# Probabilities of four heads laid out by key block, in an encoder-decoder on one core

## The chip, the cores and the metric

The kernel runs on one core of a Trainium2 chip. The metric is the device time of one execution in microseconds, the median over several runs. A profiled execution gives the trace: what each engine did and when. TensorE (PE) multiplies matrices and turns tiles, VectorE (DVE) and ScalarE (ACT) move results out of PSUM and compute on them, GpSimd (POOL) works on data in SBUF, SyncE (SP) issues DMAs.

## The reference

One encoder layer over a context of 77 tokens and one decoder layer over 2048 tokens, for two batches, width 512, 16 heads of 32, inner width 2048, all in fp32. The decoder layer is causal self-attention with a bias by relative position, cross-attention to the encoder's output, and a feed-forward net, each with a layer norm before it and a residual after it:

```python
y = y + _mha(yn, yn, dec_sa_in_w, dec_sa_in_b, dec_sa_out_w, dec_sa_out_b, sb)   # sb: bias + causal mask
y = y + _mha(_ln(y, dec_n2_s, dec_n2_b), memory, dec_ca_in_w, ..., cb)
h = _ln(y, dec_n3_s, dec_n3_b)
y = y + (jax.nn.relu(h @ dec_ff1_w.T + dec_ff1_b) @ dec_ff2_w.T + dec_ff2_b)
```

In `_mha` the scores of a head are q times k over the square root of 32, plus the bias; a softmax over the keys gives the probabilities; these times v give the head's output. The change touches the self-attention alone.

## The kernel before

**Two parts in time.** Until about 1720 us the kernel does the self-attention of both batches, with the encoder and the first cross-attention between. From there to the end it does the other cross-attentions and the feed-forward nets, with block matrices multiplied by a scheme of sums (L1376, L1405). All order is written out by hand: instructions reach each engine in the order in which the program calls them, and each engine works its queue in that order.

**Units.** The self-attention is cut into 128 units (b, m, g, t): batch, token block of 512 queries (m = 0 to 3), group of four heads, tile of 128 queries, numbered in that order, so 16 units make a token block. Unit (b, m, g, t) has m * 4 + t + 1 key blocks of 128 keys, since attention is causal: 1 to 4 in token block 0, 13 to 16 in token block 3. Units 16, 32 and 48 begin token blocks 1, 2 and 3 of batch 0; unit 64 begins batch 1, and 80, 96 and 112 its later blocks.

**A unit's steps.**

- *Scores* (`scores`, L374). A unit's key blocks go in pieces of up to four. A piece is one matmul for each of the four heads into its own PSUM bank, of the seven that go round (`bank`). VectorE moves each head's piece into the tile of probabilities `pp` and takes its maximum (L383); the last two key blocks of the unit get the bias on the way (L390).
- *Exponentials* (L400, L405). After the last piece the maxima are joined, and ScalarE does one exponential for each head, in place over all its key blocks. They are kept in a list (`late_exps`) and issued one by one at chosen places (`exps`).
- *Turns* (`turn`, L425). TensorE transposes each 128 x 128 tile of probabilities, four to a bank; ScalarE (L431) and VectorE (L429) copy the banks to SBUF. The turns of a unit go in groups of two pieces. In token block 0 four turns of one head's key blocks share a bank, elsewhere the four heads of one key block.
- *Values* (`values`, L442). The turned tiles times v, summed over the key blocks.

**Where the probabilities lie.** `pp` holds two units at once: units of even number from its start, of odd number up to its end (`probabilities`, L345). Each unit has room for (m + 1) * 512 keys for each of four heads. A head's row is contiguous: head r begins at r * (m + 1) * 512, so the places depend on m.

**The loop** (L1610). For each group of turns of unit n: if scores of n are still to be done, they are done; exponentials of n still in the list are issued; then the turns; then, behind the last group of a unit, the slot of the next one, which holds other work such as projections (L216, L227, L240) in a table by unit; then one score piece, if it may go; an exponential or two; the values; then more pieces as long as they may. `may_score` (L1593) decides whether the next piece of the stream may go. It takes the place of unit n - 2, the last of the same parity. Within one token block a piece waits only until those key blocks of n - 2 have been turned which it will write over. Where n - 2 lies in another token block or batch, it waits until all of n - 2 has been turned:

```python
same = n >= 2 and units[n][:2] == units[n - 2][:2]
return n < 2 or turned_to[n - 2] >= (min(k0 + kn, size[n - 2]) if same else size[n - 2])
```

**The ring of weights.** The last part's weights come through a ring of 16 tiles in the first half of `pp` (`w_ring`, L1271). `feed` fills it. Its first calls come during the turns of unit 126, the last of even number, for as many tiles as key blocks have been turned.

Of the kernel before, what the change touches and what calls it, by code (L numbers as in the profile page):

```python
# [12 lines left out]
ALU = mybir.AluOpType  # L13
# [4 lines left out]
P = 128  # L18
B, T, S, D = 2, 2048, 77, 512
# [3 lines left out]
HC = P // HD  # L23
MB = 512
NMB = T // MB
TB = MB // P
# [3 lines left out]
LOWEST = -3.0e38  # L30
# [24 lines left out]
def tile_encoder_decoder(ctx: ExitStack, tc: tile.TileContext, ins, out):  # L55
    nc = tc.nc
    x, src = ins["x"], ins["ctx_1024"]
# [10 lines left out]
    ident = const.tile([P, P], F32, name="ident")  # L68
# [90 lines left out]
    with (  # L159
# [9 lines left out]
        pp = ac.tile([P, 2 * HC * T], F32, name="pp")  # L169
# [10 lines left out]
        def bank():  # L180

            i = count["bank"] % count["banks"]
            count["bank"] += 1
            return psum[:, i, :]

        def in_turn(what, tile):
            i = count[what] % tile.shape[1]
            count[what] += 1
            return tile[:, i, :]

        def rows4(r):
            return slice(r * HD, (r + 1) * HD)


        nTs, qTs, ots, sums_of = {}, {}, {}, {}
# [134 lines left out]
        units = [(b, m, g, t) for b in range(B) for m in range(NMB) for g in range(NC) for t in range(TB)]  # L330
        stream = [(n, k0, kn) for n, u in enumerate(units) for k0, kn in pieces(u[1] * TB + u[3])]
        state = {}
        biases = {}
# [11 lines left out]
        def probabilities(n):  # L345
            w = (units[n][1] + 1) * MB
            at = END - HC * w if n % 2 else 0
            return [pp[:, at + r * w : at + (r + 1) * w] for r in range(HC)]

        late_exps = []  # L350

        def exps(k):

            for _ in range(min(k, len(late_exps))):
                late_exps.pop(0)[1]()

        def scores(n, k0, kn):
            b, m, g, t = units[n]
            i = m * TB + t
            if k0 == 0:  # L360
                state[n] = {
                    "p": probabilities(n),
                    "mx": sm.tile([P, HC, 8], F32, name="mx", tag="mx"),
                    "nm": sm.tile([P, HC], F32, name="nm", tag="nm"),
                    "col": 0,
                }
                if t == 0:
                    sums_of[b, m, g] = sm.tile([P, TB, HC], F32, name="sums", tag="sums")
            st = state[n]
            last = k0 + kn == i + 1  # L370
            q = qTs[b, m, g]
            banks = [bank() for _ in range(HC)]
            for r in range(HC):
                nc.tensor.matmul(  # L374
                    banks[r][:, : kn * P], q[rows4(r), ts(t, P)], kT[rows4(r), g, k0 * P : (k0 + kn) * P],
                    start=True, stop=True,
                )
            far = max(0, kn - 2) if last else kn
            col = st["col"]
            for r in range(HC):  # L380
                p, s, c = st["p"][r], banks[r], col
                if far:
                    nc.vector.tensor_scalar(  # L383
                        p[:, k0 * P : (k0 + far) * P], s[:, : far * P], 1.0, None, ALU.mult, ALU.max,
                        accum_out=st["mx"][:, r, c : c + 1],
                    )
                    c += 1
                if last:
                    w = (kn - far) * P
                    nc.vector.tensor_tensor_reduce(  # L390
                        p[:, (i + 1) * P - w : (i + 1) * P], s[:, far * P : kn * P],
                        biases[b, m, g][:, r, 2 * P - w :], 1.0, LOWEST, ALU.add, ALU.max,
                        accum_out=st["mx"][:, r, c : c + 1],
                    )
                    c += 1
            st["col"] = c
            if not last:
                return

            nc.vector.tensor_reduce(st["nm"], st["mx"][:, :, :c], AX.X, ALU.max, negate=True)  # L400
            for r in range(HC):
                p, nm, to = st["p"][r][:, : (i + 1) * P], st["nm"][:, r : r + 1], sums_of[b, m, g][:, t, r : r + 1]

                def run(p=p, nm=nm, to=to):
                    nc.scalar.activation(p, p, AF.Exp, bias=nm, accum_out=to)  # L405

                late_exps.append((n, run))
# [3 lines left out]
        def turn(pieces):  # L411

            first = units[pieces[0][0]][1] == 0
            loads = []
            for n, k0, kn in pieces:
                ks = range(k0, k0 + kn)
                if first:
                    loads += [[(n, k, r) for k in ks] for r in range(HC)]
                else:
                    loads += [[(n, k, r) for r in range(HC)] for k in ks]  # L420
            for o, load in enumerate(loads):
                pt = bank()
                pts = in_turn("pts", pts_all).rearrange("p (x q) -> p x q", q=P)
                for x, (n, k, r) in enumerate(load):
                    nc.tensor.transpose(pt[:, ts(x, P)], state[n]["p"][r][:, ts(k, P)], ident)  # L425
                    got[n, k, r] = pts[:, x, :]
                w = len(load) * P
                if o % 2 if first else o >= (len(loads) + 1) // 2:
                    nc.vector.tensor_copy(pts[:, : len(load), :], pt[:, :w])  # L429
                else:  # L430
                    nc.scalar.copy(pts[:, : len(load), :], pt[:, :w])  # L431
                if not first and o == min(3, len(loads) - 1):
                    exps(1)
            exps(HC if first else 1)
# [501 lines left out]
        for x, (b, m) in enumerate(blocks):  # L936
# [28 lines left out]
            for g in range(NC):  # L965
# [4 lines left out]
                at = u + g * TB - 3  # L970
# [78 lines left out]
        low, high = pp[:, : END // 2], pp[:, END // 2 :]  # L1049
# [208 lines left out]
        def weight_tiles():  # L1258
            for x in range(len(blocks)):
                for n in range(per):  # L1260
                    if x + 1 < len(blocks):
                        yield from cross_tiles(n)
                    if n < FIRST:
                        j, f = first_slots[n]
                        yield w1_tile(ONE[j][0], f)
                    else:
                        j, part = divmod(n - FIRST, 4)
                        for k in range(2 * part, min(2 * part + 2, 7)):
                            yield w2_d[ON_W2[TWO[j][1]], k]

        w_ring = [low[:, j % 4 * T + j // 4 * D : j % 4 * T + j // 4 * D + D] for j in range(16)]  # L1271
        tiles, fed, used = weight_tiles(), [0], [0]

        def feed(upto):
# [314 lines left out]
        size = [m * TB + t + 1 for b, m, g, t in units]  # L1589
        turned_to, scored_to, at = {n: 0 for n in range(end)}, {}, [0]  # L1590

        def may_score():

            if at[0] == len(stream):
                return False
            n, k0, kn = stream[at[0]]
            same = n >= 2 and units[n][:2] == units[n - 2][:2]
            return n < 2 or turned_to[n - 2] >= (min(k0 + kn, size[n - 2]) if same else size[n - 2])

        def score_next():  # L1600
            n, k0, kn = stream[at[0]]
            scores(n, k0, kn)
            scored_to[n] = k0 + kn
            at[0] += 1
# [4 lines left out]
        i = 0  # L1609
        while i < len(stream):  # L1610
            n = stream[i][0]
            pair = [p for p in stream[i : i + 2] if p[0] == n]
            while scored_to.get(n) != size[n]:
                score_next()
            while any(u == n for u, _ in late_exps):
                exps(1)
            ends = pair[-1][1] + pair[-1][2] == size[n]
            if ends:
                for f in ahead[n + 1]:
                    f()  # L1620
            turn(pair)
            if n == end - 2:
                for _, k0, _ in pair:
                    feed(k0 + 4)
            turned_to[n] = pair[-1][1] + pair[-1][2]
            if ends and n + 1 < end:
                slot(n + 1)
            if may_score():
                score_next()
            exps((0, 2, 1, 1)[units[n][1]])  # L1630
            for p in pair:
                values(*p)
            while may_score() and (len(pair) > 1 or units[n][1] == 0):
                score_next()
            i += len(pair)
# [67 lines left out]
```

## Time and profile before

| | |
|---|---|
| median of 3 runs | 2796.83 us (2796.19 to 2797.98) |
| profiled execution | 2796.27 us |
| its span | 2794.2 us |
| mean granted clock of TensorE | 0.997 |
| TensorE busy | 2764.6 us, 99% |
| VectorE busy | 1858.0 us, 66% |
| ScalarE busy | 1435.3 us, 51% |
| GpSimd busy | 875.6 us, 31% |

A row of a timeline gives the start, the length, the engine, the line, the operation, what it writes and reads, the shape of one, how many were merged, and in brackets how long the engine had been idle before and what released it. Rows of the same line that follow each other are merged, also when their shapes differ; the shape shown is that of the first. The profile lists a score matmul of L374 as two records, so a piece of four heads is x8. Ends of matmuls are modelled, and the distance between two starts is the safer measure. A row of windows gives a stretch, its length, and for each engine the busy time and the number of instructions, then the granted clock of TensorE and the load of the DMA engines. A row of groups gives the busy time in total, the mean length of one, and the idle time ahead of the group.

### The profile page before, as it was taken

Reading aid. Unit: us, or ns where it says so; the run is one execution under the profiler, and the core shown is the slowest. Engines: PE = TensorE matmul, PEld = TensorE weight load, DVE = VectorE, ACT = ScalarE, POOL = GpSimd, SP = SyncE. Lnnn points to the kernel's source line nnn. Section 1 sums busy time; section 2 is a strip of 40 time slices with the busy share of each in tenths; the row PEclk is TensorE's granted clock in tenths of the full one; section 3 lists DMA queues with packets and bytes.
Section 4 is the critical chain, followed back from the end, with each engine's and each line's share of the span. In section 5 each row is a group of like instructions: output and inputs, shape, how many; then the busy total and the mean of one; then the engine's idle time right before and its main releaser. Section 6 shows DMA issues by size and latency. Waiting matters only on the chain. (4 is left out here: it accounts for less than half of the span.)

```text
span 2794.2 us, 65938 instructions
## 1 busy us (share of the span) xinstructions
PE 2764.6 (99%) x25998; PEld 2076.6 (74%) x25998; DVE 1858.0 (66%) x5360; ACT 1435.3 (51%) x2751; POOL 875.6 (31%) x745
## 2 busy tenths in 40 slices
PE   9999999999999999999999999999999999999998
PEld 5567666666666556666666667898989898989898
DVE  5666587778887577687778885565555656464645
ACT  3544466656666556666646666434344444444431
POOL 0301143300100312122200001364747474746456
PEclk9999999999999999999999999999999999999999
DMA  6414344411112512232311014574747565656475
GB/s 194 116 56 135 111 143 123 139 31 48 38 41 73 140 47 70 84 107 92 106 33 39 26 50 134 174 242 145 237 152 236 175 226 163 223 162 220 148 226 181
DMA packets 281271, 355.31 MB, mean 127 GB/s; under 512 B 37968, under 2 KB 156544, under 8 KB 280834
## 3 DMA queue, kind: packets, MB, share of 16 engines
q1 hardware_dynamic: 280962, 351.10, 40.6%
q8 instruction: 206, 3.38, 0.5%
q14 instruction: 103, 0.84, 0.1%
HBM read 309.51 MB, written 41.49 MB: 126 GB/s over the span
## 5 line engine op out<-in xcount | busy, mean ns | idle before, releaser
L405 ACT ACTIVATE pp<-pp,nm 128x128 f32<-128x128 f32 (+15 forms) x512 | 612.0, 1203 | 137.2 <-DVE nm L400 136.8
L383 DVE TENSOR_SCALAR_CACHE_REDUCE pp<-psum 128x512 f32<-128x512 f32 (+3 forms) x1024 | 559.5, 591 | 64.0 <-PE psum L374 62.0
L431 ACT COPY pts<-psum 128x512 f32<-128x512 f32 (+3 forms) x592 | 300.5, 577 | 505.6 <-PE psum L425 369.7
L425 PEld LDWEIGHTS psum<-ident,pp 128*128 128x128 f32 x4352 | 473.1, 141 | 107.8 <-DVE pp L383 51.6
L425 PE MATMUL psum<-ident,pp 128*128 128x128 f32 x4352 | 533.6, 277 | 8.4 <-ACT pp L405 2.9
L429 DVE COPY pts<-psum 128x512 f32<-128x512 f32 (+2 forms) x544 | 330.0, 660 | 69.2 <-PE psum L425 67.7
L374 PE MATMUL psum<-kT,q 32*128 32x512 f32 (+3 forms) x2560 | 355.7, 576 | 5.2 <-DVE pp L383 2.6
L442 PEld LDWEIGHTS psum<-pts,vv 128*32 128x32 f32 x8704 | 225.6, 110 | 123.7 <-issue 115.8
L1405 PE MATMUL psum<-pp 128*128 128x128 f32 x2560 | 304.5, 276 | 1.9 <-POOL pp L1113 1.6
L1405 PEld LDWEIGHTS psum<-pp 128*128 128x128 f32 x2560 | 296.3, 192 | 8.6 <-issue 2.8
L442 PE MATMUL psum<-pts,vv 128*32 128x128 f32 x8704 | 278.2, 275 | 0.7 <-ACT pts L431 0.5
L1113 POOL TENSOR_TENSOR pp<-pp 128x512 f32<-128x512 f32 x159 | 212.5, 1353 | 111.1 <-DMA pp<-in_dec_ff_wT_dram 52.0
L1376 PE MATMUL psum<-vv,pp 128*128 128x256 f32 x1024 | 236.2, 381 | 0.0
L374 PEld LDWEIGHTS psum<-kT,q 32*128 32x128 f32 x2560 | 123.2, 183 | 140.7 <-issue 91.2
L1376 PEld LDWEIGHTS psum<-vv,pp 128*128 128x128 f32 x1024 | 190.3, 190 | 25.8 <-issue 0.5
L390 DVE CUSTOM_DVE_ANT_0 pp<-psum,bias 128x256 f32<-128x256 f32 (+1 forms) x512 | 196.0, 411 | 15.3 <-PE psum L374 15.2
L1389 DVE TENSOR_TENSOR kT<-kT,psum 128x512 f32<-128x512 f32 x96 | 65.8, 686 | 190.7 <-PE psum L1376 190.5
L1376 PE MATMUL psum<-nT,pp 128*128 128x256 f32 x768 | 174.1, 380 | 0.0
L1392 ACT ACTIVATE kT<-kT,vecs 128x256 f32<-128x256 f32 x192 | 87.0, 501 | 156.7 <-DVE kT L1389 156.0
L287 POOL TENSOR_TENSOR rstd<-rstd,mhalf 128x1 f32<-128x1 f32 x32 | 18.5, 578 | 458.7 <-DVE rstd L286 378.6
L1376 PEld LDWEIGHTS psum<-nT,pp 128*128 128x128 f32 x768 | 144.2, 190 | 20.3 <-issue 1.6
L470 POOL TENSOR_TENSOR oT<-rirows,oT 128x512 f32<-128x512 f32 x30 | 38.6, 1287 | 363.8 <-DMA rirows<-rec 187.8
(211 smaller groups left out, 3784.8 us busy)
## 6 DMA issues: line engine op xcount, KB each, us to landing
pp<-w_d SPq DMA_DIRECT2D x520, 256.0 KB
pp<-in_dec_ff_wT_dram SPq DMA_DIRECT2D x112, 256.0 KB
wqk<-in_dec_sa_in_wT_dram SPq DMA_DIRECT2D x64, 256.0 KB
bias<-tzg SPq DMA_DIRECT2D x128, 128.0 KB
pp<-wo_d SPq DMA_DIRECT2D x56, 256.0 KB
wbig<-in_dec_sa_in_wT_dram SPq DMA_DIRECT2D x8, 1024.0 KB
vv<-in_enc_ff_wT_dram SPq DMA_DIRECT2D x8, 1024.0 KB
xr<-in_x_dram SPq DMA_DIRECT2D x32, 256.0 KB
```

The source lines that it names most:

```text
L374: nc.tensor.matmul(banks[r][:, : kn * P], q[rows4(r), ts(t, P)], kT[rows4(r), g, k0 * P : (k0 + kn) * P], start=True, stop=True,)
L383: nc.vector.tensor_scalar(p[:, k0 * P : (k0 + far) * P], s[:, : far * P], 1.0, None, ALU.mult, ALU.max, accum_out=st["mx"][:, r, c : c + 1],)
L390: nc.vector.tensor_tensor_reduce(p[:, (i + 1) * P - w : (i + 1) * P], s[:, far * P : kn * P], biases[b, m, g][:, r, 2 * P - w :], 1.0, LOW ...
L405: nc.scalar.activation(p, p, AF.Exp, bias=nm, accum_out=to)
L425: nc.tensor.transpose(pt[:, ts(x, P)], state[n]["p"][r][:, ts(k, P)], ident)
L429: nc.vector.tensor_copy(pts[:, : len(load), :], pt[:, :w])
L431: nc.scalar.copy(pts[:, : len(load), :], pt[:, :w])
L442: nc.tensor.matmul(ot[rows4(r), t, :], vv[:, k, ts(g * HC + r, HD)], got.pop((n, k, r)), start=(k == 0), stop=(k == i),)
L1113: engine.tensor_tensor(out, a, b, ALU.subtract)
L1376: nc.tensor.matmul(mm[:, ts(f, TOK)], a[:, c, ts(f, P)], b[:, c, :], start=fresh and f == 0 and c == 0, stop=c == 1, skip_group_check=True,)
L1392: nc.scalar.activation(dst[:, e, :], src[:, e, :], AF.Relu, bias=vec("dec_ff1_b", f + e))
L1405: nc.tensor.matmul(psum[:, bank_i, ts(col, P)], lhs[:, c, :], w[:, c, :], start=fresh and k in (0, 3) and c == 0, stop=c == 3, skip_group_ ...
```

## The change

The probabilities of a unit are laid out by key block: key block k takes 512 adjacent places, 128 for each of the four heads side by side, so key block k of a unit of even number lies at k * 512 whatever the token block is. A unit of odd number still ends at the end of `pp`; when the token block grows by one, its key block k lies where key block k - 4 of the earlier unit lay, and when a new batch begins, where key block k + 12 lay. A head's row is then a row of runs of 128 elements, 512 apart, and the instructions that write or read it (L383, L390, L405) get an access pattern with one dimension more. The turns read the same 128 x 128 tiles at other places.

`may_score` has one rule for all units: a piece may go when the key blocks of unit n - 2 whose places it takes have been turned. For units of odd number at the start of a batch the shift is added (`moved`); where the token block grows, a piece waits for as many key blocks as before the shift. The slots of the ring of weights are now the 16 runs of 512 one after another, so that slot j takes the place of key block j.

```diff
         def probabilities(n):
             w = (units[n][1] + 1) * MB
             at = END - HC * w if n % 2 else 0
-            return [pp[:, at + r * w : at + (r + 1) * w] for r in range(HC)]
+            p = pp[:, at : at + HC * w].rearrange("p (k r x) -> p r k x", r=HC, x=P)
+            return [p[:, r] for r in range(HC)]
...
             for r in range(HC):
-                p, s, c = st["p"][r], banks[r], col
+                p, s, c = st["p"][r], banks[r].rearrange("p (k x) -> p k x", x=P), col
                 if far:
                     nc.vector.tensor_scalar(
-                        p[:, k0 * P : (k0 + far) * P], s[:, : far * P], 1.0, None, ALU.mult, ALU.max,
+                        p[:, k0 : k0 + far], s[:, :far], 1.0, None, ALU.mult, ALU.max,
                         accum_out=st["mx"][:, r, c : c + 1],
                     )
                     c += 1
                 if last:
-                    w = (kn - far) * P
+                    near = biases[b, m, g][:, r, :].rearrange("p (k x) -> p k x", x=P)
                     nc.vector.tensor_tensor_reduce(
-                        p[:, (i + 1) * P - w : (i + 1) * P], s[:, far * P : kn * P],
-                        biases[b, m, g][:, r, 2 * P - w :], 1.0, LOWEST, ALU.add, ALU.max,
+                        p[:, k0 + far : i + 1], s[:, far:kn], near[:, 2 - (kn - far) :], 1.0, LOWEST, ALU.add, ALU.max,
                         accum_out=st["mx"][:, r, c : c + 1],
                     )
...
             for r in range(HC):
-                p, nm, to = st["p"][r][:, : (i + 1) * P], st["nm"][:, r : r + 1], sums_of[b, m, g][:, t, r : r + 1]
+                p, nm, to = st["p"][r][:, : i + 1], st["nm"][:, r : r + 1], sums_of[b, m, g][:, t, r : r + 1]
...
-                    nc.tensor.transpose(pt[:, ts(x, P)], state[n]["p"][r][:, ts(k, P)], ident)
+                    nc.tensor.transpose(pt[:, ts(x, P)], state[n]["p"][r][:, k], ident)
...
-        w_ring = [low[:, j % 4 * T + j // 4 * D : j % 4 * T + j // 4 * D + D] for j in range(16)]
+        w_ring = [low[:, ts(j, D)] for j in range(16)]
...
             n, k0, kn = stream[at[0]]
-            same = n >= 2 and units[n][:2] == units[n - 2][:2]
-            return n < 2 or turned_to[n - 2] >= (min(k0 + kn, size[n - 2]) if same else size[n - 2])
+            if n < 2:
+                return True
+            moved = TB * max(0, units[n - 2][1] - units[n][1]) if n % 2 else 0
+            return turned_to[n - 2] >= min(k0 + kn + moved, size[n - 2])
```

## The prediction

> **What bounds the kernel now.** I read the page first, then the table of windows by unit, then TensorE's timeline around the changes of token block, and last the groups by form for the instructions whose access changes.
>
> ```profile
> span 2794.2 us, 65938 instructions
> ...
> PE 2764.6 (99%) x25998; PEld 2076.6 (74%) x25998; DVE 1858.0 (66%) x5360; ACT 1435.3 (51%) x2751; POOL 875.6 (31%) x745
> ```
>
> TensorE is never idle for long, so only time that it loses inside its own queue can be won. Its listed idle time hides some of this, because a matmul that waits in the pipe is drawn as a long one. So I compare like with like: the units of self-attention. A unit is one tile of 128 queries for one group of four heads; unit 48 is the first of token block 3 in batch 0, unit 112 the first of token block 3 in batch 1. A unit's window runs from its first turn (L425) to the next unit's.
>
> ```profile
> core 0: us, PE busy (x) PEld busy (x) DVE busy (x) ACT busy (x) POOL busy (x), PEclk, DMA share, GB/s
> ...
> 582.51:594.79 12.28, 12.28 (x152) 8.77 (x148) 7.06 (x24) 9.24 (x14) 0.00 (x0) 1.00 0.00 1
> ...
> 611.00:635.44 24.44, 22.88 (x225) 14.11 (x221) 20.00 (x62) 12.41 (x18) 1.29 (x1) 1.00 0.20 56
> 635.44:653.19 17.75, 17.75 (x212) 11.66 (x208) 15.21 (x50) 11.12 (x15) 0.00 (x0) 1.00 0.01 2
> ...
> 706.09:723.84 17.75, 17.75 (x212) 11.66 (x208) 16.23 (x53) 11.12 (x15) 3.88 (x3) 1.00 0.00 1
> ...
> 1450.14:1476.54 26.40, 24.84 (x225) 16.16 (x221) 20.08 (x62) 12.46 (x18) 1.29 (x1) 0.87 0.18 51
> ...
> 582.51:653.19 70.68, 69.07 (x764) 45.44 (x760) 55.82 (x176) 40.96 (x58) 1.29 (x1) 1.00 0.07 21
> 1421.65:1494.29 72.64, 71.03 (x764) 47.48 (x761) 55.91 (x176) 41.17 (x58) 1.29 (x1) 0.95 0.07 20
> ```
>
> The rows are units 46, 48, 49, 53 and 112, then units 46 to 49 and 110 to 113 together. Units 48 and 112 take 24.44 and 26.40 us where their neighbours take 17.75. Part of that is honest work: scores of unit 49 that could not be issued earlier. The rest is loss, and the next two fences price it. First a unit without a passage (52), as the price list; a cost is the distance between two starts, since the ends are modelled:
>
> ```profile
> 688.85 0.71 PE L374 MATMUL psum<-kT,q 32*128 32x256 f32 x8
> 689.49 3.71 PE L425 MATMUL psum<-ident,pp 128*128 128x128 f32 x32
> 693.14 1.14 PE L374 MATMUL psum<-kT,q 32*128 32x512 f32 x8
> 694.21 1.95 PE L442 MATMUL psum<-pts,vv 128*32 128x128 f32 x64
> ...
> 697.16 2.40 PE L425 MATMUL psum<-ident,pp 128*128 128x128 f32 x20
> 699.40 3.60 PE L216 MATMUL psum<-nT,wqk 128*128 128x512 f32 x8
> ...
> 705.23 0.93 PE L374 MATMUL psum<-kT,q 32*128 32x384 f32 x8
> ```
>
> So a score piece of four key blocks costs 1.07 us (693.14 to 694.21), of three 0.86 (705.23 to 706.09, where the next unit's window begins), of two 0.64 (688.85 to 689.49); 32 turns cost 3.65, 20 turns 2.24. Now the passage from unit 47 to 49:
>
> ```profile
> 592.93 1.14 PE L374 MATMUL psum<-kT,q 32*128 32x512 f32 x8
> ...
> 601.39 2.26 PE L374 MATMUL psum<-kT,q 32*128 32x384 f32 x16
> 603.58 1.97 PE L425 MATMUL psum<-ident,pp 128*128 128x128 f32 x16
> ...
> 611.00 0.55 PE L425 MATMUL psum<-ident,pp 128*128 128x128 f32 x3
> 612.78 3.38 PE L425 MATMUL psum<-ident,pp 128*128 128x128 f32 x29 [1.23 <-ACT pp L405]
> 616.09 1.14 PE L374 MATMUL psum<-kT,q 32*128 32x512 f32 x8
> ...
> 619.05 1.58 PE L374 MATMUL psum<-kT,q 32*128 32x512 f32 x14
> 620.96 5.14 PE L374 MATMUL psum<-kT,q 32*128 32x256 f32 x18 [0.33 <-DVE pp L383]
> 626.03 2.66 PE L425 MATMUL psum<-ident,pp 128*128 128x128 f32 x20
> 628.65 3.70 PE L240 MATMUL psum<-wbig,nT 128*128 128x512 f32 x8
> ```
>
> Four places lose time. (a) Two pieces in a row, of three and two blocks: 601.39 to 603.58 is 2.19 against 0.86 + 0.64 = 1.50, a loss of 0.69. (b) The first 32 turns of unit 48: 611.00 to 616.09 is 5.09 against 3.65, a loss of 1.44, and the row names the exponential. (c) Four pieces in a row (x14 and x18 records are 4 x 8; three of four blocks, one of two): 619.05 to 626.03 is 6.98 against 3 x 1.07 + 0.64 = 3.85, a loss of 3.13, and the row names VectorE's evacuation L383. (d) 20 turns: 2.62 against 2.24, a loss of 0.38. Together 5.64 us. The second passage has the same work and is longer by 72.64 - 70.68 = 1.96, so it loses 7.60. The extra is the clock:
>
> ```profile
> 1462.00:1470.00 8.00, 8.00 (x35) 6.12 (x34) 6.63 (x26) 2.15 (x4) 0.00 (x0) 0.57 0.01 2
> ...
> 1466.12 3.89 PE L425 MATMUL psum<-ident,pp 128*128 128x128 f32 x20
> 1469.85 3.60 PE L240 MATMUL psum<-wbig,nT 128*128 128x512 f32 x8
> ```
>
> Right behind the starved stretch the granted clock is 0.57 over 8 us, and the same 20 turns take 3.73.
>
> **The change part by part.** *Order.* Before, a piece of a unit in a new token block waited until the unit two earlier was turned completely; now it waits only for the key blocks whose place it takes. Following the loop of L1610 with both rules, the order differs at three places in 128 units. At 46 to 49, and alike at 110 to 113, unit 48's pieces 0 and 4 move from unit 47 into unit 46 (behind its first eight blocks of turns, around its products), piece 8 moves ahead of unit 47, piece 11 follows unit 47's turns, and unit 49's pieces 0 and 4 follow in unit 47, piece 8 ahead of unit 48. Unit 48 then has 49's last piece, 50's 0 and 4, each behind turns or products, which is the pattern of unit 52. At 62 to 64 unit 64's one block is scored a half unit earlier; no row there shows a wait for it, and I price it at nothing, hidden by unit 63's two groups of turns. The passages from block 0 to 1 and 1 to 2 do not change: those units have at most eight key blocks and turn them in one go, so there is no earlier moment. Nothing is added or removed: the same turns, pieces, products and projections lie between the start of unit 46 and that of unit 50, so the whole difference is loss removed.
>
> *Loss (c), (a) and (d).* They arise because VectorE gets several pieces at once:
>
> ```profile
> L383 DVE TENSOR_SCALAR_CACHE_REDUCE pp<-psum 128x512 f32<-128x512 f32 x672 | 422.8, 687 | 48.0 <-PE psum L374 47.4
> ...
> L383 DVE TENSOR_SCALAR_CACHE_REDUCE pp<-psum 128x256 f32<-128x256 f32 x128 | 53.8, 420 | 6.8 <-PE psum L374 6.8
> L383 DVE TENSOR_SCALAR_CACHE_REDUCE pp<-psum 128x384 f32<-128x384 f32 x96 | 47.8, 554 | 7.3 <-PE psum L374 6.2
> ...
> L816 DVE TENSOR_TENSOR pts<-psum,cmx 128x308 f32<-128x308 f32 x52 | 24.9, 479 | 2.3
> ...
> L1386 ACT COPY kT<-psum 128x512 f32<-128x512 f32 x96 | 57.4, 598 | 91.0 <-PE psum L1376 90.9
> ...
> L431 ACT COPY pts<-psum 128x512 f32<-128x512 f32 x544 | 283.2, 594 | 455.5 <-PE psum L425 325.7 <-DVE oT L448 71.7 <-issue 24.3
> ```
>
> A head's evacuation occupies 422.8 / 672 = 0.63 us, a piece of four heads 2.52, while TensorE makes it in 1.07; with seven banks TensorE is one and a half pieces ahead at most. Spread out, the same 55.82 us of VectorE in 70.68 become 55.82 / (70.68 - 5.64) = 86%, as in unit 49 (15.21 of 17.75, 86%) and below unit 53 (16.23 of 17.75, 91%), both without such a wait. Unit 46, where VectorE is only 7.06 of 12.28 busy, takes in three pieces in place of most of one (made from 592.93 on, so some 1.7 us of its evacuation lies before the window's end at 594.79): about 7.06 - 1.7 + 2 x 2.52 + 4 x 0.50 = 12.4 in 12.28 + 1.07 + 0.86 = 14.2 us, 87%. What is queued behind them there is one copy of turned blocks, and TensorE has a projection of 3.60 us to do meanwhile.
>
> *Loss (b).*
>
> ```profile
> 604.32 1.07 ACT L431 COPY pts<-psum 128x512 f32<-128x512 f32 x2 [6.78 <-PE psum L425]
> 605.95 1.68 ACT L405 ACTIVATE pp<-pp,nm 128x1664 f32<-128x1664 f32 x1 [0.56 <-DVE nm L400]
> ...
> 610.97 1.67 ACT L405 ACTIVATE pp<-pp,nm 128x1664 f32<-128x1664 f32 x1
> ```
>
> All four exponentials of unit 48 run between 605.95 and 612.64 and the turns of the fourth head wait for the last. With the new order the first of them is called before unit 47's last turns. Three are left, without the wait for the maxima: behind the two copies that end at 605.39 they are done near 605.4 + 3 x 1.67 = 610.4, and unit 48's turns begin at 611.0. That cover of 0.6 us is TensorE's projection and products between; if it is gone, the 1.44 comes back as far as it is short.
>
> *Layout.* Rows of probabilities become runs of 128 elements with a hop of 512. Turns still read 128 adjacent columns, so TensorE is untouched. For VectorE, L816 writes four runs of 77 (three hops): 479 ns, where the line between 420 (256) and 554 (384) gives 474 at 308. So 5 ns, 1.7 a hop. For ScalarE, L1386 writes two runs of 256: 598 against 594. With 13 to 16 runs in each of four exponentials that is at most 4 x 15 x 4 ns = 0.24 us a unit, on an engine busy 11.12 of 17.75. Both are hidden. Ends: nothing, and, at the other side, a hop as dear as an instruction of its own (rival 2). No gain is to be had from hops, since the element count stays. The ring of weights for the last stage gets other slots in the same half of the buffer, filled at the same four calls; a slot is one run of 512 either way, so nothing.
>
> *Sum.* 5.64 + 7.60 = 13.24 us at most. I leave 0.3 at each passage for small bank waits: 12.6. The profiled execution took 2796.27 us, so 2783.7; the median of the runs is 0.56 above it. I predict 2784 us. Bounds: all of it and a little more, 2781 to 2783; half of it, 2790.
>
> **The rivals.** 1. *The wait moves.* VectorE works in order, and the early evacuations go ahead of copies that TensorE needs. For it: unit 46 rises to 87%. Against it: units 49 and 53 carry as much. Time: half the gain, 2787 to 2793, about 2790.
>
> 2. *Hops cost* (the slower side). Place: L383 and L390 in every unit of token block 3 (32 units; 13 to 16 blocks in four or five instructions for each of four heads make 36 to 44 hops, say 40). VectorE has 17.75 - 15.21 = 2.54 us to spare, 64 ns a hop; above that each 10 ns costs 0.40 us a unit, 12.8 in all, so the change loses from about 75 ns. The upper price is the fixed part of an instruction: 687 - 420 is 267 ns for 256 elements, so 420 - 267 = 153 ns. At 153: (6.1 - 2.54) x 32 = 114 us, which with the forecast's gain makes 2898 us. Against it: 1.7 ns in L816.
>
> 3. *The change does nothing*, because these passages are bound by VectorE's total and not by its timing: 2796 to 2797. Against it: VectorE is 79% busy over units 46 to 49 (55.82 of 70.68).
>
> 4. *The dip of the clock is no part of the passage.* The second passage loses 1.96 us more only through the 0.57; if that comes in some executions and not in others, each passage is worth 5.64, and 2 x 5.64 - 0.6 = 10.7 gives 2786. For it: the same starved stretch left the clock at 1.00 in the first passage. Against it: the times shown for this kernel lie within 2796.19 to 2797.98, so it does not come and go by much more. The Trainium skill, "TensorE: Matmul & The Clock Gate", Part 1, says that the array's clock is halved after an idle window of about 3.4 us, and that this window runs free of the kernel. By that rule the dip is luck of the phase, and the two passages' rows agree with it.
>
> **How the numbers follow.** About 0.2%, 5.6 us, is what can be told from no change. Forecast, both passages cleared with the clock's part (2781 to 2785.5): 0.60. Cleared without it (about 2786): 0.14. Wait moves: 0.10, two thirds of it below 2791.2. Nothing: 0.06. Hops, or a wait of the new order that I do not see: 0.10. Faster 0.81, same 0.09, slower 0.10. So faster is 0.60 + 0.14 + 0.07. The range 2781 to 2792 holds the first two and most of the moved wait; the slow ends are left out.
>
> **What would show it.** Units 48 and 112 near 17.5 us, unit 46 near 14.2, units 46 to 49 and 110 to 113 near 65 each with the clock at 1.00; no wait of L425 for L405 at unit 48; L383 at 128x512 still within 10 ns of 687 and L405 at 1664 elements within 30 ns of 1.67 us; every other unit and the last stage unchanged. Wrong would be: longer L383 or L405 rows (rival 2), or units 46 and 47 longer by what 48 loses (rival 1).

## The result, and the profile after

| | before | after |
|---|---|---|
| median | 2796.83 us (2795.94 to 2798.52, 7 runs) | 2788.22 us (2787.28 to 2788.93, 7 runs) |
| ratio | | 0.9968, 95% interval 0.9956 to 0.9979 |
| span of the profiled execution | 2794.2 us | 2785.3 us |

The change gains 8.6 us, where 12.6 were forecast. Lines have moved by one in the kernel after: the score matmul is L375 in place of L374, the moves to the probabilities are L384 and L391 in place of L383 and L390. The first fence is from the page of the kernel after, the second its windows by unit: units 46, 47, 48, 49 and 112, then 46 to 49 and 110 to 113 together.

```profile
PE 2760.4 (99%) x25998; PEld 2072.2 (74%) x25998; DVE 1859.1 (67%) x5360; ACT 1436.4 (52%) x2751; POOL 876.6 (31%) x745
```

```profile
582.68:596.89 14.21, 14.21 (x168) 9.39 (x164) 11.94 (x40) 9.36 (x14) 0.00 (x0) 1.00 0.01 1
596.89:613.75 16.86, 16.86 (x189) 10.75 (x185) 13.55 (x43) 9.90 (x14) 0.00 (x0) 1.00 0.01 2
613.75:632.29 18.54, 18.54 (x209) 11.70 (x205) 15.11 (x46) 10.81 (x15) 1.29 (x1) 1.00 0.25 74
632.29:650.04 17.75, 17.75 (x212) 11.66 (x208) 15.20 (x50) 11.13 (x15) 0.00 (x0) 1.00 0.01 2
1448.87:1467.41 18.54, 18.54 (x208) 11.70 (x204) 15.11 (x46) 10.81 (x15) 1.29 (x1) 1.00 0.25 73
582.68:650.04 67.36, 67.36 (x764) 43.50 (x760) 55.81 (x176) 41.19 (x58) 1.29 (x1) 1.00 0.07 22
1417.71:1485.17 67.46, 67.45 (x765) 43.51 (x761) 55.81 (x176) 41.18 (x58) 1.29 (x1) 1.00 0.08 21
```

The two passages (units 46 to 49 and 110 to 113) went from 70.68 to 67.36 us and from 72.64 to 67.46, together 8.50 us. That is nearly all of the 8.9 us between the two spans, and the granted clock is 1.00 in both. Unit 112 fell from 26.40 to 18.54 us. But 65 us each were expected. TensorE's timeline of units 47 and 48 after the change shows what is left:

```profile
600.54 0.71 PE L375 MATMUL psum<-kT,q 32*128 32x256 f32 x8
601.18 1.95 PE L442 MATMUL psum<-pts,vv 128*32 128x128 f32 x64
603.07 3.03 PE L375 MATMUL psum<-kT,q 32*128 32x512 f32 x16
606.03 2.05 PE L425 MATMUL psum<-ident,pp 128*128 128x128 f32 x16
...
613.75 3.71 PE L425 MATMUL psum<-ident,pp 128*128 128x128 f32 x32
617.39 0.71 PE L375 MATMUL psum<-kT,q 32*128 32x256 f32 x8
618.03 1.96 PE L442 MATMUL psum<-pts,vv 128*32 128x128 f32 x64
619.92 3.03 PE L375 MATMUL psum<-kT,q 32*128 32x512 f32 x16
622.88 2.66 PE L425 MATMUL psum<-ident,pp 128*128 128x128 f32 x20
```

The wait for the exponential is gone: the first 32 turns of unit 48 take 617.39 - 613.75 = 3.64 us. The four pieces in a row are gone too. In their place stand two pairs: x16 records are two full pieces back to back, and each pair takes 2.96 us (603.07 to 606.03, 619.92 to 622.88) where two single pieces take 2.14. Nothing in TensorE's idle column says so; the pair is merely drawn long. The turns behind the pairs are slow too: 20 turns take 2.62 us (622.88 to 625.50, where the projection L240 starts), as before the change and against 2.24 in unit 52, and 16 turns take 2.00 (606.03 to 608.03) against 1.80 before (603.58 to 605.38).

### The profile page after: what moved, and what is told of

Same layout as the page of the kernel before. It is cut to its first block, busy times and chain, and to the rows that moved or that the text cites. A ratio compares the mean times of both kernels' runs of the same rounds, so it can differ in the third digit from the quotient of the medians.

```text
span 2785.3 us, 65935 instructions
## 1 busy us (share of the span) xinstructions
PE 2760.4 (99%) x25998; PEld 2072.2 (74%) x25998; DVE 1859.1 (67%) x5360; ACT 1436.4 (52%) x2751; POOL 876.6 (31%) x745
## 5 line engine op out<-in xcount | busy, mean ns | idle before, releaser
L405 ACT ACTIVATE pp<-pp,nm 128x128 f32<-128x128 f32 (+15 forms) x512 | 612.0, 1203 | 150.2 <-DVE nm L400 141.7
L384 DVE TENSOR_SCALAR_CACHE_REDUCE pp<-psum 128x512 f32<-128x512 f32 (+3 forms) x1024 | 559.4, 591 | 66.7 <-PE psum L375 65.3
L425 PEld LDWEIGHTS psum<-ident,pp 128*128 128x128 f32 x4352 | 471.2, 141 | 106.6 <-DVE pp L384 54.7
L425 PE MATMUL psum<-ident,pp 128*128 128x128 f32 x4352 | 531.9, 277 | 6.0 <-ACT nT L311 2.3
L375 PE MATMUL psum<-kT,q 32*128 32x512 f32 (+3 forms) x2560 | 351.5, 574 | 4.4 <-DVE pp L384 1.9
L375 PEld LDWEIGHTS psum<-kT,q 32*128 32x128 f32 x2560 | 118.6, 183 | 139.1 <-issue 92.6
L391 DVE CUSTOM_DVE_ANT_0 pp<-psum,bias 128x256 f32<-128x256 f32 (+1 forms) x512 | 196.1, 411 | 15.1 <-PE psum L375 15.0
```

The lines of the kernel that those rows point to most:

```text
L375: nc.tensor.matmul(banks[r][:, : kn * P], q[rows4(r), ts(t, P)], kT[rows4(r), g, k0 * P : (k0 + kn) * P], start=True, stop=True,)
L384: nc.vector.tensor_scalar(p[:, k0 : k0 + far], s[:, :far], 1.0, None, ALU.mult, ALU.max, accum_out=st["mx"][:, r, c : c + 1],)
L391: nc.vector.tensor_tensor_reduce(p[:, k0 + far : i + 1], s[:, far:kn], near[:, 2 - (kn - far) :], 1.0, LOWEST, ALU.add, ALU.max, accum_out ...
L425: nc.tensor.transpose(pt[:, ts(x, P)], state[n]["p"][r][:, k], ident)
```

## The experiments

Each experiment has the kernel before measured beside it on the same chip. Its medians there are 2797.06 us (layout alone, one passage, both spreadings), 2798.39 (exponentials held back, six banks) and 2797.12 (freed order without the layout).

### Is it the order or the layout?

The layout alone: the kernel after with the old condition.

```diff
-            moved = TB * max(0, units[n - 2][1] - units[n][1]) if n % 2 else 0
-            return turned_to[n - 2] >= min(k0 + kn + moved, size[n - 2])
+            same = n >= 2 and units[n][:2] == units[n - 2][:2]
+            return n < 2 or turned_to[n - 2] >= (min(k0 + kn, size[n - 2]) if same else size[n - 2])
```

> The new layout alone: rows of probabilities as runs of 128, but a piece at a change of token block waits again until the unit two earlier is turned completely, so every queue has the order of before. If the gain came from the order alone and a hop costs next to nothing: 2796.8 us as before (2795 to 2798), VectorE's moves of 128x512 still 687 ns, the exponential of 1664 elements 1.67 to 1.70 us, units 48 and 112 at 24.4 and 24.4 to 26.4 us. If hops cost something that the new order hides: over 2799 us and longer rows. If the layout itself brought a part of the 8.6 us: under 2794 us.

Measured: 2798.16 us, ratio 1.0004 (0.9996 to 1.0013). The groups of VectorE's moves and of the exponential over 13 key blocks, then the latter in the kernel before, then the window of units 46 to 49 with the layout alone:

```profile
L384 DVE TENSOR_SCALAR_CACHE_REDUCE pp<-psum 128x512 f32<-128x512 f32 x672 | 422.8, 687 | 48.2 <-PE psum L375 47.9
...
L405 ACT ACTIVATE pp<-pp,nm 128x1664 f32<-128x1664 f32 x32 | 53.9, 1696 | 1.2 <-DVE nm L400 1.2
```

```profile
L405 ACT ACTIVATE pp<-pp,nm 128x1664 f32<-128x1664 f32 x32 | 53.9, 1697 | 1.1 <-DVE nm L400 1.1
```

```profile
584.04:654.77 70.73, 69.07 (x764) 45.44 (x761) 55.81 (x176) 40.97 (x58) 1.28 (x1) 1.00 0.08 21
```

Hops cost nothing that can be seen: 687 ns as before with three hops to an instruction, 1696 ns with twelve, where one contiguous run took 1697. The passage loses as much as before. So the layout by itself brings nothing, and the gain comes with the order. That the old places do not permit this order is read from the code, where a key block of unit 48 comes to lie over other heads and key blocks of unit 46; no run tries it.

### One passage alone

The new condition up to unit 65, the old one from there.

```diff
+            if n >= 66 and units[n][:2] != units[n - 2][:2]:
+                return turned_to[n - 2] >= size[n - 2]
```

> The changed kernel with the new rule up to unit 65 only: batch 0's change to token block 3 and the change of batch keep the new order, batch 1's change to token block 3 (units 110 to 113) has the order of before. Theory: each passage is worth 3.3 us by its waits, the second up to 1.96 more by the clock, and the change of batch 0.8. Then 2796.8 - 3.3 - 0.8 = 2792.7 us. If the dip of the clock is part of the second passage, unit 112 takes 26.4 us as in the trace of before; if it is luck of the phase, 24.4 us or between, with the clock at 1.00.

Measured: 2793.07 us, ratio 0.9984 (0.9975 to 0.9993), 4.0 us below the kernel before (2 to 7 by the interval), where 4.1 were expected. Its windows of units 46 to 49, 110 to 113 and 112:

```profile
582.89:650.25 67.36, 67.36 (x764) 43.54 (x760) 55.82 (x176) 41.18 (x58) 1.28 (x1) 1.00 0.08 22
1417.53:1490.74 73.21, 71.54 (x765) 47.78 (x761) 55.96 (x176) 41.17 (x58) 1.29 (x1) 0.95 0.08 20
1446.02:1472.98 26.96, 25.34 (x224) 16.43 (x221) 20.23 (x62) 12.68 (x19) 1.29 (x1) 0.87 0.19 50
```

The first passage takes 67.36 us as with the whole change. The second, left with the old order, is starved as before: TensorE waits for the exponential and for banks. The clock dips in it again. So the gain adds up passage by passage.

### Is the dip of the clock part of the second passage?

The kernel before was traced twice more, unchanged.

> The kernel before once more, for the clock. If the dip of the clock belongs to the starved stretch of unit 112 and not to unit 48's, this trace has it again within 8 to 15 us of unit 112's start and unit 112 takes 26 to 27 us, unit 48 24.4. If it is luck of the phase, it is missing in unit 112 or comes in unit 48 too in one of the two repeated traces.

> The same as the other repetition of the kernel before: with the dip a part of the second passage, unit 112 at 26 to 27 us and unit 48 at 24.4; with luck of the phase, another pattern in one of the two.

The windows of units 48 and 112 in the first repetition, then in the second:

```profile
610.74:635.18 24.44, 22.88 (x224) 14.11 (x221) 19.99 (x62) 12.42 (x18) 1.29 (x1) 1.00 0.21 56
1450.42:1474.86 24.44, 22.87 (x225) 14.10 (x221) 19.99 (x62) 12.42 (x18) 1.29 (x1) 1.00 0.20 55
```

```profile
612.49:638.89 26.40, 24.84 (x224) 16.17 (x221) 20.08 (x62) 12.46 (x18) 1.29 (x1) 0.87 0.20 52
1453.01:1477.45 24.44, 22.87 (x225) 14.10 (x221) 19.99 (x62) 12.41 (x18) 1.29 (x1) 1.00 0.19 55
```

In the first neither unit has a dip; in the second it is in the other passage. Over the five traces with a starved passage (before, its two repetitions, the layout alone, one passage alone) the clock dipped in four of nine, and unit 48 or 112 then took 1.96 us (26.40 against 24.44) to 2.52 us (26.96) more. The second of the layout alone, 26.71 us at a clock of 0.87, is the fourth. So the dip does not belong to the second passage; a starved stretch takes it or not from execution to execution. The single runs took 2795.27 us without a dip in these units and 2797.82 us with one. The Trainium skill, "TensorE: Matmul & The Clock Gate", Part 1, has the clock decided in windows that run free of the kernel. These rows agree in that the same code dips in some executions only; where the windows lie, they do not show. The Trainium skill names in the same part an idle window of about 3.4 us as what halves the clock, and that does not fit these traces. The longest idle time named in the starved stretch of the kernel before is 1.23 us, and by the single records of its trace no two matmuls that follow each other start more than 1.51 us apart there. Still the clock fell to half in the second passage:

```profile
1464.00:1466.00 2.00, 2.00 (x8) 0.50 (x2) 2.00 (x9) 0.00 (x0) 0.00 (x0) 0.50 0.00 0
```

One more stretch dips, outside the change: from 108 to 124 us the mean granted clock is 0.79 both before and after, and 0.68 in both repetitions. Being the same in the two executions compared, it is no part of the 8.9 us between their spans; it may add to the spread of the times.

### Why two pieces in a row lose

Six banks going round in place of seven, run once:

```diff
-        count = {"bank": 0, "banks": 7, "pts": 0, "oT": 0, "mm": 0}
+        count = {"bank": 0, "banks": 6, "pts": 0, "oT": 0, "mm": 0}
```

> The changed kernel with six PSUM banks going round in the self-attention in place of seven. If two full pieces in a row lose their 0.82 us because the last head's bank is not yet emptied, one bank less makes them wait for one evacuation more, 0.63 us: the pair in unit 47 goes from 2.96 to about 3.6 us, and single pieces stay at 1.07. If VectorE's total is the limit, the pair stays within 0.1 us of 2.96.

The same pair in unit 47, and a single full piece behind it:

```profile
621.87 3.64 PE L375 MATMUL psum<-kT,q 32*128 32x512 f32 x16
625.45 2.05 PE L425 MATMUL psum<-ident,pp 128*128 128x128 f32 x16
...
631.08 1.14 PE L375 MATMUL psum<-kT,q 32*128 32x512 f32 x8
632.15 1.08 PE L442 MATMUL psum<-pts,vv 128*32 128x128 f32 x32
```

The pair takes 625.45 - 621.87 = 3.58 us, 0.62 more than with seven banks, which is one evacuation of a head (0.63); the single piece stays at 1.07. A pair wants eight banks and waits for VectorE to empty the missing ones. In the kernel after, with seven, TensorE's weight loads (PEld) for the pair's last head show it; they wait until VectorE has emptied the first bank:

```profile
604.22 0.69 DVE L384 TENSOR_SCALAR_CACHE_REDUCE pp<-psum 128x512 f32<-128x512 f32 x1 [0.83 <-PE psum L375]
...
604.98 0.29 PEld L375 LDWEIGHTS psum<-kT,q 32*128 32x128 f32 x2 [0.75 <-DVE pp L384]
```

The turns behind a pair take their banks from the same seven (`turn` calls `bank`) and wait in the same way. In the single records of the trace the last four of the 16 begin at 607.42 us, right behind an evacuation that ends at 607.36, and the last two fours of the 20 at 624.28 and 624.89, behind two that end at 624.21 and 624.82. The whole kernel with six took 2844.03 us, so the seventh bank is worth far more than these pairs.

### Pieces spread out at the passages

Pieces may also go behind the products of the single last piece of a unit, where the token block changes two units on:

```diff
-            while may_score() and (len(pair) > 1 or units[n][1] == 0):
+            passes = n + 2 < end and units[n][:2] != units[n + 2][:2]
+            while may_score() and (len(pair) > 1 or units[n][1] == 0 or passes):
```

> The changed kernel, where the last unit of even and of odd number of a token block may issue one more score piece behind its single last piece's products. Unit 48's last piece then goes ahead of unit 47's turns and unit 49's ahead of unit 48's, so no two full pieces follow each other in these units. Theory: the 2.3 us that each passage still loses (2.96 us for two full pieces in a row against 2 x 1.07 in unit 47 and again in unit 48, and the turns behind them) come from eight banks wanted at once where seven go round. Then unit 47 falls from 16.85 to 15.7 us, unit 48 from 18.54 to 17.4, and the time by about 4.4 us, to 2783.8 us. Rival: VectorE's total work is the limit in these units. Then units 46 to 49 together stay at 67.4 us, the loss shows elsewhere in them, and the time stays at 2788 us.

Measured: 2783.92 us, ratio 0.9953 (0.9941 to 0.9966). Units 47 and 48, and 46 to 49:

```profile
598.04:613.77 15.73, 15.73 (x188) 10.36 (x185) 13.55 (x43) 9.79 (x14) 0.00 (x0) 1.00 0.02 3
613.77:631.02 17.25, 16.97 (x201) 10.98 (x197) 14.46 (x44) 10.96 (x15) 1.29 (x1) 1.00 0.28 79
583.19:648.77 65.58, 65.30 (x764) 42.71 (x760) 55.80 (x176) 41.23 (x58) 1.29 (x1) 1.00 0.08 22
```

The time is near the 2783.8 us expected. The passage falls to 65.58 us with VectorE's work unchanged (55.80 us). It was the timing of the pieces, not VectorE's total.

### Pieces spread out everywhere, and a miss

```diff
-            while may_score() and (len(pair) > 1 or units[n][1] == 0):
+            while may_score():
```

> The same freedom in every unit: pieces go behind any products as soon as their place is turned. Beside the two passages this separates the pairs of full pieces in the second unit of each head group of token block 2, eight units, where the trace of before shows 2.97 us (398.33 to 401.30) against 2 x 1.07. Theory of the seven banks: 8 x 0.83 = 6.6 us more than the kernel with the passages alone, 2777 us, and those units at 14.6 in place of 15.45 us. Rival, VectorE's total: no gain beyond that kernel, or a loss where pieces come too early.

Measured: 2816.52 us, ratio 1.0066 (1.0052 to 1.0080): slower by 19 us where 20 us of gain were expected. Unit 34 took 18.06 us in place of 13.79. Its rows on TensorE and ScalarE, and its window:

```profile
407.50 3.28 PE L425 MATMUL psum<-ident,pp 128*128 128x128 f32 x28
...
410.15 1.58 ACT L405 ACTIVATE pp<-pp,nm 128x1536 f32<-128x1536 f32 x1 [5.98 <-DVE nm L400]
411.73 2.03 ACT L431 COPY pts<-psum 128x512 f32<-128x512 f32 x4
412.35 0.66 PE L425 MATMUL psum<-ident,pp 128*128 128x128 f32 x4 [1.57 <-ACT pts L431]
```

```profile
407.50:425.56 18.06, 16.49 (x168) 10.72 (x164) 11.56 (x40) 9.35 (x14) 12.30 (x11) 0.91 0.55 158
```

The pieces went earlier, so the list of exponentials ran a unit ahead, and the loop issued one of unit 35 in the middle of unit 33. Its maxima were not ready. ScalarE stood still for 5.98 us, until 410.15, and the copies of unit 34's turns, which begin at 407.50, came only behind the exponential, at 411.73. TensorE ran out of banks after 28 turns, which fill seven, and the clock dipped (0.91). The Trainium skill, "TensorE: Matmul & The Clock Gate", Architectural detail: the array is 16× 32×32, not 1× 128×128, calls ScalarE's and VectorE's queues strict first in, first out; the row agrees. The test is the same kernel with the exponentials held back:

```diff
             for _ in range(min(k, len(late_exps))):
+                if late_exps[0][0] > turning[0] + 1:
+                    return
                 late_exps.pop(0)[1]()
...
-            n = stream[i][0]
+            n = turning[0] = stream[i][0]
```

> The kernel with free pieces in every unit, but during unit n no exponential of unit n + 2 is issued. Theory from that kernel's trace: its 19 us of loss come from ScalarE's order. Unit 35's first exponential was issued during unit 33, waited 5.98 us for its maxima, and the copies of unit 34's turns stood behind it, so unit 34 took 18.06 us in place of 13.79. Then the third unit of each head group of token block 2 falls back to 13.8 to 14.2 us and the time to that of the kernel with the passages alone, 2784 us, or up to 6 us below. Rival: the pieces themselves come too early and take VectorE from the copies. Then it stays above 2805 us.

Measured: 2773.62 us, ratio 0.9911 (0.9897 to 0.9924), the fastest kernel of this study. Unit 34, and units 32 to 45 in this kernel; then units 32 to 45 of the kernel with the passages alone:

```profile
409.23:423.02 13.79, 13.79 (x169) 9.40 (x165) 11.29 (x40) 9.35 (x14) 6.97 (x8) 1.00 0.73 210
...
381.45:578.89 197.44, 197.44 (x2205) 127.96 (x2205) 158.31 (x517) 124.29 (x204) 67.36 (x56) 1.00 0.49 142
```

```profile
380.30:583.19 202.89, 202.89 (x2205) 132.96 (x2205) 158.76 (x517) 124.11 (x204) 67.37 (x56) 1.00 0.47 139
```

Unit 34 is back at 13.79 us, and units 32 to 45 gain 5.45 us, those of batch 1 about as much. That is more than the up to 6 us expected for both batches. The pairs in the second unit of a head group, which were the reason to expect it, bring 1.1 to 1.2 us in each of units 33, 37, 41 and 45; units 35, 39 and 43 bring 0.7 each, which the expectation had not counted and which the kernel without the held-back exponentials does not show; unit 32 costs 1.1.

### The freed order without the new layout

The kernel before with the same two edits.

> The kernel before, with its own layout and its rule for changes of token block, and with the two edits of the best version: pieces go behind any products as soon as they may, and during unit n no exponential of unit n + 2 is issued. Theory: the 10.8 us that those edits brought in token block 2 (units 32 to 45 and 96 to 109, 202.9 to 197.4 us each) need no new layout, and the two passages stay starved, since unit 48 still waits for unit 46 and unit 49 for unit 47: 2797 - 10.8 = 2786 us, units 46 to 49 still near 70.7 us (72.6 with a dip of the clock). If the new layout is needed for the gain in token block 2 too: 2795 us or more. If the freed order alone also mends the passages: under 2780 us.

Measured: 2792.00 us, ratio 0.9984 (0.9975 to 0.9993). Units 32 to 45, 46 to 49 and 110 to 113, and two rows of TensorE in units 46 and 47:

```profile
380.82:578.25 197.43, 197.43 (x2204) 127.94 (x2204) 158.34 (x517) 124.41 (x204) 67.47 (x56) 1.00 0.49 143
578.25:652.37 74.12, 74.03 (x764) 49.11 (x761) 56.00 (x176) 41.05 (x58) 1.27 (x1) 0.95 0.08 20
1415.24:1489.52 74.28, 74.19 (x765) 49.56 (x761) 55.83 (x176) 41.36 (x58) 1.27 (x1) 0.95 0.07 20
```

```profile
590.54 5.50 PE L376 MATMUL psum<-kT,q 32*128 32x512 f32 x24
...
608.92 6.53 PE L376 MATMUL psum<-kT,q 32*128 32x512 f32 x24
```

Token block 2 gains the same without the layout, as expected. The passages get worse than before, 74.12 against 70.68 and 74.28 against 72.64, which was not expected, and the kernel misses the expected 2786 us: once unit 46 is turned, three pieces of unit 48 go in a row (590.54), and three of unit 49 after unit 47 (608.92), and the clock dips in both passages (0.95), so that a part of the first difference is the clock's. With the layout and its condition the same two edits give 2773.62. So with these edits the change is worth some 18 us (2792.00 against 2773.62; the kernels before beside them differ by 1.3), against 8.6 as it came. No run parts the layout from its condition here.

## Why the prediction was right, and where it was short

*Direction and range.* Faster, and 2788.22 lies in 2781 to 2792; the gain is 8.6 of 12.6 us.

*The step that was mis-sized* is the order: "Unit 48 then has 49's last piece, 50's 0 and 4, each behind turns or products, which is the pattern of unit 52." It is not that pattern. The small last pieces take the places behind the turns, and pieces 0 and 4 of units 49 and 50 follow each other behind the products. I left 0.3 us at each passage for bank waits; the passages stand at 67.36 and 67.46 where 65.04 (70.68 - 5.64) would be free of loss, 2.3 and 2.4. The two pairs make 2 x 0.82 of that, the 20 turns 0.38 and the 16 turns 0.20. Spreading the pairs takes 1.78 of it away (67.36 to 65.58), and 0.54 stays. The share of VectorE over four units (86%) was no argument: what counts is how many banks are wanted at one place.

*Loss (b)*, the exponentials: right. No wait of L425 for L405 is left at unit 48. *Losses (a), (c), (d)*: the cause was right, VectorE gets several pieces at once. But two pairs come in the place of (a) and (c), and loss (d), the slow 20 turns of unit 48, was counted as won and is there unchanged, 2.62 us before and after.

*Unit 46*: 14.21 us, as forecast (14.2), with VectorE at 11.94 of it, 84% (87% forecast). Its length is what it had before plus the prices of the two pieces more (12.28 + 1.07 + 0.86), so nothing was held up there. Rival 1 (the wait moves, 2787 to 2793) has the time right and the mechanism wrong: a wait did move, but into units 47 and 48, and it is for banks that hold scores, not for copies. *Rival 3* (nothing) is ruled out by the result.

*Hops* (rival 2): nothing, 687 and 1696 ns.

*The clock* (rival 4): right as a rival. The sum put 1.96 us on the second passage; they came in that execution by chance. With four dips in nine starved passages, I estimate that a kernel with two of them takes about one such dip an execution, so some 2 us do belong to the gain, but to neither passage. The term thus comes out about right in size, and that is luck. I took the closeness of the times shown for evidence against the rival, and that was too weak: later runs of the kernel before spread from 2794.02 to 2802.5 us.

*Units 62 to 64*: priced at nothing. Unit 62 took 15.38 us against 15.82; the projection L216 waits 0.16 us for ScalarE's copies, as the first row shows of after, and 0.55 before, as the second shows:

```profile
867.23 3.70 PE L216 MATMUL psum<-nT,wqk 128*128 128x512 f32 x8 [0.16 <-ACT pts L431]
```

```profile
870.38 3.70 PE L216 MATMUL psum<-nT,wqk 128*128 128x512 f32 x8 [0.55 <-ACT pts L431]
```

No run takes this part alone. Its 0.4 us is read from traces: unit 62 takes 15.38 to 15.39 us after and with either spreading or the held-back exponentials, and 15.82 in each trace with the old rule that was compared (before, its first repetition, the layout alone, the freed order without the layout).

## What to carry to other kernels

Where a matmul unit is 99% busy, compare the distance between starts with the same instructions in an undisturbed place; a queue that waits for banks is drawn as long matmuls, not as idle time. When work is let go earlier, count the buffers wanted at each place of the new order, not the mean load, and look at what else the earlier work lets go: here exponentials that then blocked copies in an in-order queue. A change of layout that is worth nothing by itself can be worth much with the order that it permits.

## What was unexpected of the hardware

The clock of TensorE falls to half (0.50 from 1464 to 1466 us) in a stretch in which TensorE keeps getting work, with no named idle time above 1.23 us, and it does so in some executions only: four of nine starved passages, at 2 to 2.5 us each. A pair of full pieces lost 0.82 us with seven banks and 1.44 us with six, 0.62 more for the bank less, which is one evacuation. An access pattern with a hop of 512 elements after every 128 cost neither VectorE nor ScalarE anything in these rows: 687 and 1696 ns, against 687 and 1697.
